# A two-layer graph kernel: the last 20 rows taken as a block of 128, and the third pair of logits parted evenly

## The chip, the cores and the metric

The kernel runs on one core of one Trainium2 chip. The metric is the device time in microseconds (us) of one execution; less is better. A core has the engines TensorE (PE, with its weight load PEld), VectorE (DVE), ScalarE (ACT), GpSimd (POOL) and SyncE (SP, which issues transfers). Each works through its own queue of instructions in order, and the queues meet only at semaphores. On-chip memory is SBUF (128 partitions) and PSUM, where TensorE puts its products.

## The reference

There are N = 2708 nodes with 256 features, an adjacency matrix `adj` (2708 x 2708, some 0.3% of it not zero), and two layers. Everything is 32-bit floating point.

```
x  = layernorm(x + relu([x, adj @ x] @ weight + bias))          # layer 0
R  = (adj + I) / row sums                                       # layer 1
Xf = Xa = x
for n in 0, 1:
    A  = top_p_attention(Xa)     # softmax of q k^T, kept to 0.9 of each row's mass, renormed
    Xf = R @ Xf
    Xa = A @ Xa
    Z  = Z + Xf @ U1[n].T + Xa @ U2[n].T
x  = layernorm(x + layernorm(x + Z) * g + b)
```

with `q = X W1^T W2^T` and `k = X W3^T`, both of 64 features. The attention is over all pairs of nodes: two matrices of 2708 x 2708.

## The kernel before, in words

The nodes are cut into NB = 22 blocks: 21 of 128 rows and one, EDGE, of 20 (2708 = 21 x 128 + 20). `rows(k)` gives 128 or 20. A product over all nodes is 22 matmuls that add up in PSUM, the last one over 20 rows only. Each 32-bit matmul appears in the trace as two MATMUL and two LDWEIGHTS records.

Stages, in time: up to 28 us x is projected to `y0` (L392 to L399). **Layer 0** (28 to 285 us) goes over blocks m: `adj_product` (L257) multiplies 22 tiles of adj, loaded by SP, with `y0`; then comes the projection of x itself (L462), and DVE does relu and layernorm. Every fourth block `x1_qk` (L426) makes the queries q and the keys. Keys of even chunks of 512 columns lie on partitions 0 to 63, those of odd chunks on 64 to 127, so that the two matmuls of a pair of logits use different rows of the array. Six chunks make three pairs, the third of 512 and 148 columns.

Meanwhile DVE collects which columns of each adjacency block are not empty, and `Lists.end` (L325 to L348) turns these lists into indices: a transfer out and in, then seven scatters by POOL (L345), each after the one before has landed, and a load of the result, `ix<-list_d` (L348). There are two such lists; the first comes between layer 0 and the attention.

**Step 0 of the attention** (286 to 722 us). `begin1` starts blocks 0 to 2: logits (`logits`, L507) are copied by ACT (L514) to a row block `e`, with projections by U1 (L651) between. `extract1` (DVE: L570, L577, L579) finds the largest logits, `exps1` (ACT: L611, L613) makes exponentials, and `finish1` (DVE: L627 to L640) cuts at 0.9 of the mass. Then, for each block t, six turns g: `turn` transposes four blocks of e (L527), ACT copies them to `wT` (L530, and L533 for the 20-row one), and `products`, one turn later, multiplies them with x1 (L564). The last turn has two blocks, 20 and 21; its products come in the next block's first turn. Between them stand the logits of block t+3. The order is the program's, written out by hand; no scheduler changes it. POOL gathers pieces of adj (L367).

**Step 1** (from 748 us) has periods `per` of the same kind: transposes, products with `ya` (L564 again), the logits of a later block (L507), a search for the threshold on ACT (L966, L969) and DVE (L1023, L1030, L1083, L1088), and, between them in equal parts, the sparse products R @ X (`r_units`, L749). For these POOL gathers rows by index (`y_load`, L719), seven gathers per block, into two buffers, one block ahead. From about 1047 us POOL also does part of the final normalization (L1207, L1208), which waits for ACT's L1192.

The line of the product in a turn:

```
nc.tensor.matmul(acc[:p, :D], lhsT=wT[:kw, k % 4, :p], rhs=y[:kw, k, :],
                 start=k == 0, stop=k == NB - 1)
```

with kw = 20 where k = 21. For the EDGE block of step 1, `edge_product` (L544 to L550) does all in one.

Of the kernel before, what the change touches and what calls it, by code (L numbers as in the profile page):

```python
# [38 lines left out]
CAP = 160  # L39
ML = 16  # L40
CW, CC = 128, 7


def chunks(N):
    return [(a, min(N, a + CH)) for a in range(0, N, CH)]


class Common:
# [3 lines left out]
@with_exitstack  # L52
def gnn_two_layer_kernel(ctx: ExitStack, tc: tile.TileContext, N, xT_d, x_d, adj_d, w0_d, b0_d,
                         w1_d, w2_d, w3_d, u1_d, u2_d, g_d, b_d, out_d):

    nc = tc.nc
    D = x_d.shape[1]
    DA = w1_d.shape[1]  # L80
    NB = (N + P - 1) // P
    DC = D // P
    assert N % 2 == 0 and NB % 2 == 0 and N * 2.0 ** -15 < 0.09 and DC == 2 and DA == 64
    assert SEG * (NS - 1) + 8 <= N <= SEG * NS == SEG2 * NS2 and N >= SEG2 * (NS2 - 1) + 8
    assert NB == 3 * KS + 1 and CW == P and CAP % 8 == 0 and N < NB * P
# [63 lines left out]
def fast_path(ctx, tc, c, flags, fint, xT_d, x_d, w0_d, b0_d, w1_d, w2_d, w3_d, u1_d, u2_d, g_d, b_d):  # L149
# [97 lines left out]
    def adj_product(acc, m, y, n, stop):  # L247
        p = rows(m)
        halves = adj_of.pop(m)
        for k in range(NB):  # L250
            kw = rows(k)
            if m == EDGE:
                o = EW * (k % 4)
                nc.tensor.matmul(acc[o:o + p, :n], lhsT=halves[k // KH][:kw, k % KH, :p], rhs=y[:kw, k, :n],
                                 start=k < 4, stop=k >= NB - 4)
                continue
            nc.tensor.matmul(acc[:p, :n], lhsT=halves[k // KH][:kw, k % KH, :p], rhs=y[:kw, k, :n],  # L257
                             start=k == 0, stop=stop and k == NB - 1)


# [141 lines left out]


    q = big.tile([P, N], FP, tag="Q", name="q")
    keys = [big.tile([P, (len(CHS) + 1) // 2, CH], FP, tag=f"K{s}", name=f"k{s}") for s in range(2)]


    wqkq = small.tile([P, DC, 3, DA], FP, tag="wqkq", name="wqkq", bufs=1)
# [10 lines left out]
    def qk_project(s, a, b, src):  # L419


        n, i, h = b - a, a // CH // 2, a // CH % 2
        po = ps_misc()
        for j in range(DC):
            w = wqkq[:, j, 1 - h:3 - h].rearrange("p h a -> p (h a)")
            nc.tensor.matmul(po[:, :n], lhsT=w, rhs=src(j), start=j == 0, stop=j == DC - 1)  # L426
        own, other = (slice(DA * g, DA * g + DA) for g in (h, 1 - h))
        nc.scalar.copy(q[other, a:b], po[other, :n])
        nc.scalar.copy(q[own, a:b], po[other, :n])
        nc.scalar.copy(keys[s][own, i, a % CH:a % CH + n], po[own, :n])  # L430

    x1T = big.tile([P, DC, N], FP, tag="B", name="x1T")

# [63 lines left out]
    NL = (len(CHS) + 1) // 2  # L497

    def logits(s, t, i):


        p = rows(t)
        lg = ps_lg()
        cs = CHS[2 * i:2 * i + 2]
        for h, (a, b) in enumerate(cs):
            o = slice(DA * h, DA * h + DA)
            nc.tensor.matmul(lg[:p, h, :b - a], lhsT=q[o, t * P:t * P + p], rhs=keys[s][o, i, :b - a],  # L507
                             start=True, stop=True)
        a, b = cs[0][0], cs[-1][1]
        return lg.rearrange("p h n -> p (h n)")[:p, :b - a], a, b  # L510

    def logits1(t, i):
        lg, a, b = logits(0, t, i)
# [4 lines left out]
    NG = (NB + 3) // 4  # L518
    before = []

    def turn(t, g, y, acc, e):
        p = rows(t)
        ks = range(4 * g, min(NB, 4 * g + 4))
        tr = ps_tr()
        for k in ks:
            kw = rows(k)
            nc.tensor.transpose(tr[:kw, k % 4, :p], e[:p, k * P:k * P + kw], ident[:p, :p])  # L527
        wT = work.tile([P, 4, P], FP, tag="wT", name="wT", bufs=3)
        full = sum(rows(k) == P for k in ks)
        nc.scalar.copy(wT[:, :full, :p], tr[:, :full, :p])  # L530
        if full < len(ks):
            kw = rows(ks[full])
            nc.scalar.copy(wT[:kw, full, :p], tr[:kw, full, :p])  # L533
        before.append((p, ks, wT, y, acc))

    def edge_product(y, acc, e):

        p = rows(EDGE)
        tr = ps_tr().rearrange("p k i -> p (k i)")[:, :NB * p].rearrange("p (k i) -> p k i", i=p)
        wT = work.tile([P, 4, P], FP, tag="wT", name="wT", bufs=3)  # L540
        wT = wT.rearrange("p k i -> p (k i)")[:, :NB * p].rearrange("p (k i) -> p k i", i=p)
        for k in [NB - 1] + list(range(NB - 1)):
            kw = rows(k)
            nc.tensor.transpose(tr[:kw, k, :], e[:p, k * P:k * P + kw], ident[:p, :p])  # L544
        for a, b, kw in ((0, NB - 1, P), (NB - 1, NB, rows(NB - 1))):
            nc.scalar.copy(wT[:kw, a:b, :], tr[:kw, a:b, :])
        for k in range(NB):
            kw = rows(k)
            o = EW * (k % 4)
            nc.tensor.matmul(acc[o:o + p, :D], lhsT=wT[:kw, k, :], rhs=y[:kw, k, :],  # L550
                             start=k < 4, stop=k >= NB - 4)

    def products(keep):

        if len(before) > keep:
            p, ks, wT, y, acc = before.pop(0)
            for k in ks:
                kw = rows(k)
                if p < P:
                    o = EW * (k % 4)  # L560
                    nc.tensor.matmul(acc[o:o + p, :D], lhsT=wT[:kw, k % 4, :p], rhs=y[:kw, k, :],
                                     start=k < 4, stop=k >= NB - 4)
                    continue
                nc.tensor.matmul(acc[:p, :D], lhsT=wT[:kw, k % 4, :p], rhs=y[:kw, k, :],  # L564
                                 start=k == 0, stop=k == NB - 1)

    def seg_max(dst, src, p, step, width):
# [94 lines left out]
    def ya_pair():  # L662
# [11 lines left out]
        if rows(t0 + 1) == P:  # L674
            nc.scalar.copy(ya[:, t0:t0 + 2, :], pz)
            return
        for s in range(2):
            nc.scalar.copy(ya[:rows(t0 + s), t0 + s, :], pz[:rows(t0 + s), s, :])

    def step1_out(t, acc, ra):  # L680

# [215 lines left out]
    for t in range(NB):  # L897
# [6 lines left out]
        for g in range(NG):  # L904
# [16 lines left out]
            if g == 2:  # L921
# [813 lines left out]
```

## Time and profile before

| | |
|---|---|
| median of 3 runs | 1295.33 us (1294.3 to 1296.72) |
| profiled execution | 1291.2 us, of which the span of instructions 1289.4 |
| PE busy | 1226.3 us, 95% of the span |
| PEld, DVE, ACT, POOL busy | 888.1, 973.9, 735.5, 635.9 us |
| chain that ended last | PE 79%, DVE 8%, ACT 7%, DMA 3%, POOL 2% |
| products of 20 rows | 42 records each at L257 and in both steps of L564 |
| third pairs of logits (512 and 148 columns) | 22 in each step |

A row of a timeline gives the start in us, the length in us, the engine, the line, the operation, what is written `<-` what is read, the shape (for PE `rows*columns` of the array, then the moving operand) and how many instructions were merged. In brackets stands how long the engine was idle before, and what ended that; "issue" is nothing that the profile shows. Matmuls overlap, so the time that one takes of the engine is read from start to start, not from its own length.

### The profile page before, as it was taken

To read this page: it belongs to the slowest core of one execution; us is meant where nothing else is said; L and a number is where in the kernel's file an instruction comes from. 1 tells how busy PE (TensorE), PEld (TensorE's weight loads), DVE (VectorE), ACT (ScalarE), POOL (GpSimd) and SP (SyncE) were. 2 spreads that over 40 slices of the span, in tenths; PEclk is the share of its full clock that TensorE was granted. 3 is DMA by queue.
4 is the path that set the end of the run, shared out by engine and by line. 5 is a ranking of instruction groups with operands and counts; after the bars stand their busy time and mean duration, and the time that the engine had idled before them with its cause. 6 is when DMAs were issued, how large, how long until landed. Compare 5 with 4: busy or idle time off the path is not lost.

```text
span 1289.4 us, 18741 instructions
## 1 busy us (share of the span) xinstructions
PE 1226.3 (95%) x5764; PEld 888.1 (69%) x5764; DVE 973.9 (76%) x3252; ACT 735.5 (57%) x1337; POOL 635.9 (49%) x594
## 2 busy tenths in 40 slices
PE   8999999979899999999999987999999999999885
PEld 6878777843477777777777555777766777767664
DVE  2445545884999997977872179889888999999886
ACT  2000110125456656556655488887888989989822
POOL 1000000003475452577756058878874878888860
PEclk9999999999999999999999988999999999999998
DMA  7455445423322210122224244565563545565451
GB/s 196 152 193 170 143 149 168 149 90 107 121 82 83 72 57 28 43 88 91 93 85 100 63 149 150 178 189 177 180 154 118 179 155 154 165 195 158 145 139 39
DMA packets 101703, 165.99 MB, mean 129 GB/s; under 512 B 17362, under 2 KB 74070, under 8 KB 101594
## 3 DMA queue, kind: packets, MB, share of 16 engines
q1 hardware_dynamic: 75308, 108.65, 26.0%
q0 software_dynamic: 20544, 51.17, 14.3%
q10 hardware_dynamic: 5742, 4.89, 1.3%
q8 instruction: 48, 0.79, 0.2%
q14 instruction: 61, 0.50, 0.1%
HBM read 130.74 MB, written 33.90 MB: 128 GB/s over the span
## 4 chain that ended last, share of the span: by engine, by line
PE 79%; DVE 8%; ACT 7%; DMA 3%; POOL 2%; issue 2%; ACTq 0%; POOLq 0%; DVEq 0%
PE acc L564 27%; PE acc L257 16%; PE lg L507 9%; PE misc L749 8%; PE tr L527 7%; PE acc L651 2%; DMA yg<-v_d,ix 2%; PE acc L462 2%; PE misc L392 2%; PE misc L426 2%; PE acc L672 2%; ACT e L966 2%; PE misc L699 1%; DVE e L1088 1%; ACT e L844 1%
## 5 line engine op out<-in xcount | busy, mean ns | idle before, releaser
L530 ACT COPY wT<-tr 128x512 f32<-128x512 f32 (+2 forms) x258 | 132.1, 519 | 208.7 <-PE tr L527 208.7
L564 PE MATMUL acc<-x,wT 128*128 128x256 f32 (+1 forms) x924 | 230.5, 388 | 0.0
L564 PE MATMUL acc<-ya,wT 128*128 128x256 f32 (+1 forms) x924 | 227.1, 385 | 0.0
L719 POOL DMA_INDIRECT yg<-v_d,ix x154 | 194.8, 1265 | 59.6 <-issue 22.6
L564 PEld LDWEIGHTS acc<-x,wT 128*128 128x128 f32 (+1 forms) x924 | 165.2, 189 | 71.0 <-issue 37.4
L719 POOL DMA_INDIRECT yg<-yf_d,ix x154 | 188.2, 1222 | 48.3 <-issue 22.5
L257 PE MATMUL acc<-y,adj_t 128*128 128x257 f32 (+1 forms) x924 | 208.4, 381 | 0.0
L564 PEld LDWEIGHTS acc<-ya,wT 128*128 128x128 f32 (+1 forms) x924 | 170.2, 190 | 44.4 <-issue 24.0
L749 PE MATMUL misc<-yg,adj_t 128*128 128x256 f32 (+1 forms) x704 | 183.7, 394 | 14.9 <-DMA yg<-v_d,ix 5.9
L367 POOL DMA_INDIRECT adj_t<-in_adj,ix x154 | 171.3, 1112 | 52.0 <-issue 41.8
L257 PEld LDWEIGHTS acc<-y,adj_t 128*128 128x128 f32 (+1 forms) x924 | 171.8, 189 | 32.7 <-issue 8.9
L749 PEld LDWEIGHTS misc<-yg,adj_t 128*128 128x128 f32 (+1 forms) x704 | 123.6, 189 | 67.6 <-issue 23.4
L507 PE MATMUL lg<-k,q 64*128 64x512 f32 (+3 forms) x528 | 149.5, 594 | 13.7 <-ACT e L848 7.0
L527 PE MATMUL tr<-ident,e 128*128 128x128 f32 (+2 forms) x946 | 147.1, 274 | 3.1 <-DVE e L1088 2.0
L527 PEld LDWEIGHTS tr<-ident,e 128*128 128x128 f32 (+2 forms) x946 | 112.2, 138 | 44.8 <-issue 16.4
L334 POOL DMA_DIRECT2D part_d<-e x1 | 0.6, 573 | 285.6 <-DVE e L333 285.6
L439 ACT COPY x1T<-tr 128x256 f32<-128x256 f32 (+1 forms) x22 | 8.0, 364 | 186.6 <-PE tr L438 186.6
L966 ACT ACTIVATE e<-e,st 128x2708 f32<-128x2708 f32 (+1 forms) x43 | 113.5, 2639 | 0.1
L969 ACT ACTIVATE e<-e,st 128x2708 f32<-128x2708 f32 (+1 forms) x42 | 110.9, 2641 | 0.1
L570 DVE MAX8 cand<-e 128x8 f32<-128x170 f32 (+1 forms) x352 | 87.2, 318 | 26.7 <-ACT e L514 26.7
L1030 DVE MAX8 cand<-w 128x8 f32<-128x170 f32 (+1 forms) x352 | 94.2, 321 | 0.0
L1083 DVE MATCH_REPLACE8 w<-part,e 128x680 f32<-128x680 f32 (+1 forms) x88 | 74.3, 851 | 0.0
(238 smaller groups left out, 1696.4 us busy)
## 6 DMA issues: line engine op xcount, KB each, us to landing
adj_t<-in_adj SPq DMA_DIRECT2D x44, 704.0 KB
adj_t<-adjc_d SPq DMA_DIRECT2D x44, 448.0 KB
adjc_d<-adj_t SPq DMA_DIRECT2D x22, 256.0 KB
base<-za_d SPq DMA_DIRECT2D x40, 128.0 KB
adjc_d<-adj_t SPq DMA_DIRECT2D x22, 192.0 KB
xt<-in_x ACTq DMA_DIRECT2D x21, 128.0 KB
x_d<-x SPq DMA_DIRECT2D x21, 128.0 KB
x1b_d<-xb SPq DMA_DIRECT2D x21, 128.0 KB
```

The lines of the kernel that those rows point to most:

```text
L257: nc.tensor.matmul(acc[:p, :n], lhsT=halves[k // KH][:kw, k % KH, :p], rhs=y[:kw, k, :n], start=k == 0, stop=stop and k == NB - 1)
L367: nc.gpsimd.indirect_dma_start(out=a[:CW, i, :], out_offset=None, in_=adj_rows, in_offset=bass.IndirectOffsetOnAxis(ap=ix[:CW, m, i:i + 1] ...
L507: nc.tensor.matmul(lg[:p, h, :b - a], lhsT=q[o, t * P:t * P + p], rhs=keys[s][o, i, :b - a], start=True, stop=True)
L527: nc.tensor.transpose(tr[:kw, k % 4, :p], e[:p, k * P:k * P + kw], ident[:p, :p])
L530: nc.scalar.copy(wT[:, :full, :p], tr[:, :full, :p])
L564: nc.tensor.matmul(acc[:p, :D], lhsT=wT[:kw, k % 4, :p], rhs=y[:kw, k, :], start=k == 0, stop=k == NB - 1)
L570: nc.vector.max(dst[:p, i * 8:(i + 1) * 8], src[:p, i * step:i * step + w])
L719: nc.gpsimd.indirect_dma_start(out=y[:CW, i, :], out_offset=None, in_=rows_d, in_offset=bass.IndirectOffsetOnAxis(ap=ix[:CW, m, i:i + 1], ...
L749: nc.tensor.matmul(acc[:p, :D], lhsT=a[:kw, k, :p], rhs=y[:kw, k, :], start=k == 0, stop=k == CC)
L966: nc.scalar.activation(scr[:b.p, :N], e, AF.Relu, bias=b.nz, scale=b.l[k], accum_out=b.relu)
L969: nc.scalar.activation(scr[:b.p, :N], e, AF.Sign, bias=b.nz, scale=b.l[k], accum_out=b.sign)
L1030: nc.vector.max(b.cand[:p, 8 * i:8 * i + 8], low[:p, SEG2 * i:SEG2 * (i + 1)])
```

## The change

1. In layer 0, `y0`'s last block gets zeros (a memset by POOL), and `adj_product` multiplies all 128 rows of the last block.
2. In the attention the last column block is taken as columns 2592 to 2720 of `e` instead of the 20 from 2688. Its 20 real rows are then rows 96 to 115 of the transpose (AT = 96); the rest meets zeros in the other factor. For step 0 that factor is a new piece `x1_edge`, zeroed by POOL and filled with 20 rows by DVE, both after `lists.end()`; for step 1 it is `ya`'s last block, zeroed by POOL at (t, g) = (2, 0) of step 0. ACT copies both transposes of the last turn in one instruction.
3. The third pair of logits is parted into 330 and 330 columns (`key_parts`); the projections that cross the new border at 2378 are parted (columns 2048 to 2560 in layer 0, block 18 in step 0).

```diff
+def key_parts(N):
+    parts = []
+    for a in range(0, N, 2 * CH):
+        b = min(N, a + 2 * CH)
+        parts += [(a, (a + b) // 2), ((a + b) // 2, b)]
+    return parts
...
-            nc.tensor.matmul(acc[:p, :n], lhsT=halves[k // KH][:kw, k % KH, :p], rhs=y[:kw, k, :n],
+            nc.tensor.matmul(acc[:p, :n], lhsT=halves[k // KH][:, k % KH, :p], rhs=y[:, k, :n],
                              start=k == 0, stop=stop and k == NB - 1)
...
     y0 = big.tile([P, NB, D + 1], FP, tag="V", name="y0")
+    nc.gpsimd.memset(y0[:, NB - 1, :D], 0.0)
...
     def qk_project(s, a, b, src):
+        for c_, (ka, kb) in enumerate(KPS):
+            lo, hi = max(a, ka), min(b, kb)
+            if lo >= hi:
+                continue
...
     lists.end()
...
+    x1_edge = y_room[:, YW + 4 * D:YW + 5 * D]
+    nc.gpsimd.memset(x1_edge, 0.0)
+    nc.vector.tensor_copy(x1_edge[AT:AT + rows(EDGE)], x1[:rows(EDGE), EDGE, :])
     lists = Lists(ML, NB, flags[:, NF - 2:], yg[:, 1].rearrange("p c d -> p (c d)"))
...
-        cs = CHS[2 * i:2 * i + 2]
+        cs = KPS[2 * i:2 * i + 2]
+        skip = CH - (cs[0][1] - cs[0][0])
...
+    def columns(e, k):
+        a = min(k * P, NW - P)
+        return e[:, a:a + P]
+
+    def part_y(y, k):
+        return y[:, k, :] if k < NB - 1 or y is ya else x1_edge
...
         for k in ks:
-            kw = rows(k)
-            nc.tensor.transpose(tr[:kw, k % 4, :p], e[:p, k * P:k * P + kw], ident[:p, :p])
+            nc.tensor.transpose(tr[:, k % 4, :p], columns(e[:p], k), ident[:p, :p])
         wT = work.tile([P, 4, P], FP, tag="wT", name="wT", bufs=3)
-        full = sum(rows(k) == P for k in ks)
-        nc.scalar.copy(wT[:, :full, :p], tr[:, :full, :p])
-        if full < len(ks):
-            kw = rows(ks[full])
-            nc.scalar.copy(wT[:kw, full, :p], tr[:kw, full, :p])
+        nc.scalar.copy(wT[:, :len(ks), :p], tr[:, :len(ks), :p])
...
-                nc.tensor.matmul(acc[:p, :D], lhsT=wT[:kw, k % 4, :p], rhs=y[:kw, k, :],
+                nc.tensor.matmul(acc[:p, :D], lhsT=wT[:, k % 4, :p], rhs=part_y(y, k),
                                  start=k == 0, stop=k == NB - 1)
...
+            if (t, g) == (2, 0):
+                nc.gpsimd.memset(ya[:, NB - 1, :], 0.0)
```

More of the change, by code (lines that the diff above doesn't have):

```diff
@@ L41 @@
 CW, CC = 128, 7
+AT = 96
 def chunks(N):
     return [(a, min(N, a + CH)) for a in range(0, N, CH)]
+def key_parts(N):
[4 more added lines that the diff above has]
+    return parts
 class Common:
@@ L84, in gnn_two_layer_kernel @@
     assert SEG * (NS - 1) + 8 <= N <= SEG * NS == SEG2 * NS2 and N >= SEG2 * (NS2 - 1) + 8
+    assert SEG * NS - P == (NB - 1) * P - AT and AT + N - (NB - 1) * P <= P
     assert NB == 3 * KS + 1 and CW == P and CAP % 8 == 0 and N < NB * P
@@ L250, in adj_product @@
         for k in range(NB):
-            kw = rows(k)
             if m == EDGE:
                 o = EW * (k % 4)
-                nc.tensor.matmul(acc[o:o + p, :n], lhsT=halves[k // KH][:kw, k % KH, :p], rhs=y[:kw, k, :n],
+                nc.tensor.matmul(acc[o:o + p, :n], lhsT=halves[k // KH][:, k % KH, :p], rhs=y[:, k, :n],
                                  start=k < 4, stop=k >= NB - 4)
                 continue
-            nc.tensor.matmul(acc[:p, :n], lhsT=halves[k // KH][:kw, k % KH, :p], rhs=y[:kw, k, :n],
+            nc.tensor.matmul(acc[:p, :n], lhsT=halves[k // KH][:, k % KH, :p], rhs=y[:, k, :n],
                              start=k == 0, stop=stop and k == NB - 1)
@@ L404, in fast_path @@
     q = big.tile([P, N], FP, tag="Q", name="q")
-    keys = [big.tile([P, (len(CHS) + 1) // 2, CH], FP, tag=f"K{s}", name=f"k{s}") for s in range(2)]
+    KPS = key_parts(N)
+    keys = [big.tile([P, len(KPS) // 2, CH], FP, tag=f"K{s}", name=f"k{s}") for s in range(2)]
     wqkq = small.tile([P, DC, 3, DA], FP, tag="wqkq", name="wqkq", bufs=1)
@@ L419, in qk_project @@
     def qk_project(s, a, b, src):
[L422 to L430, printed above, removed]
+        for c_, (ka, kb) in enumerate(KPS):
+            lo, hi = max(a, ka), min(b, kb)
+            if lo >= hi:
+                continue
+            n, i, h = hi - lo, c_ // 2, c_ % 2
+            po = ps_misc()
+            for j in range(DC):
+                w = wqkq[:, j, 1 - h:3 - h].rearrange("p h a -> p (h a)")
+                nc.tensor.matmul(po[:, :n], lhsT=w, rhs=src(j)[:, lo - a:hi - a], start=j == 0, stop=j == DC - 1)
+            own, other = (slice(DA * g, DA * g + DA) for g in (h, 1 - h))
+            nc.scalar.copy(q[other, lo:hi], po[other, :n])
+            nc.scalar.copy(q[own, lo:hi], po[other, :n])
+            nc.scalar.copy(keys[s][own, i, lo - ka:hi - ka], po[own, :n])
     x1T = big.tile([P, DC, N], FP, tag="B", name="x1T")
@@ L495, in fast_path @@
     x1_qk(len(CHS) - 1)
-    NL = (len(CHS) + 1) // 2
+    NL = len(KPS) // 2
     def logits(s, t, i):
@@ L503, in logits @@
         lg = ps_lg()
-        cs = CHS[2 * i:2 * i + 2]
+        cs = KPS[2 * i:2 * i + 2]
+        skip = CH - (cs[0][1] - cs[0][0])
         for h, (a, b) in enumerate(cs):
             o = slice(DA * h, DA * h + DA)
-            nc.tensor.matmul(lg[:p, h, :b - a], lhsT=q[o, t * P:t * P + p], rhs=keys[s][o, i, :b - a],
+            at = (skip, 0)[h]
+            nc.tensor.matmul(lg[:p, h, at:at + b - a], lhsT=q[o, t * P:t * P + p], rhs=keys[s][o, i, :b - a],
                              start=True, stop=True)
         a, b = cs[0][0], cs[-1][1]
-        return lg.rearrange("p h n -> p (h n)")[:p, :b - a], a, b
+        return lg.rearrange("p h n -> p (h n)")[:p, skip:skip + b - a], a, b
     def logits1(t, i):
@@ L525, in turn @@
         for k in ks:
-            kw = rows(k)
-            nc.tensor.transpose(tr[:kw, k % 4, :p], e[:p, k * P:k * P + kw], ident[:p, :p])
+            nc.tensor.transpose(tr[:, k % 4, :p], columns(e[:p], k), ident[:p, :p])
         wT = work.tile([P, 4, P], FP, tag="wT", name="wT", bufs=3)
-        full = sum(rows(k) == P for k in ks)
-        nc.scalar.copy(wT[:, :full, :p], tr[:, :full, :p])
-        if full < len(ks):
-            kw = rows(ks[full])
-            nc.scalar.copy(wT[:kw, full, :p], tr[:kw, full, :p])
+        nc.scalar.copy(wT[:, :len(ks), :p], tr[:, :len(ks), :p])
         before.append((p, ks, wT, y, acc))
@@ L541, in edge_product @@
         wT = wT.rearrange("p k i -> p (k i)")[:, :NB * p].rearrange("p (k i) -> p k i", i=p)
[L542 to L546, printed above, removed]
         for k in range(NB):
-            kw = rows(k)
+            nc.tensor.transpose(tr[:, k, :], columns(e[:p], k), ident[:p, :p])
+        nc.scalar.copy(wT, tr)
+        for k in range(NB):
             o = EW * (k % 4)
-            nc.tensor.matmul(acc[o:o + p, :D], lhsT=wT[:kw, k, :], rhs=y[:kw, k, :],
+            nc.tensor.matmul(acc[o:o + p, :D], lhsT=wT[:, k, :], rhs=part_y(y, k),
                              start=k < 4, stop=k >= NB - 4)
@@ L557, in products @@
             for k in ks:
-                kw = rows(k)
                 if p < P:
                     o = EW * (k % 4)
-                    nc.tensor.matmul(acc[o:o + p, :D], lhsT=wT[:kw, k % 4, :p], rhs=y[:kw, k, :],
+                    nc.tensor.matmul(acc[o:o + p, :D], lhsT=wT[:, k % 4, :p], rhs=part_y(y, k),
                                      start=k < 4, stop=k >= NB - 4)
                     continue
-                nc.tensor.matmul(acc[:p, :D], lhsT=wT[:kw, k % 4, :p], rhs=y[:kw, k, :],
+                nc.tensor.matmul(acc[:p, :D], lhsT=wT[:, k % 4, :p], rhs=part_y(y, k),
                                  start=k == 0, stop=k == NB - 1)
@@ L676, in ya_pair @@
             return
-        for s in range(2):
-            nc.scalar.copy(ya[:rows(t0 + s), t0 + s, :], pz[:rows(t0 + s), s, :])
+        nc.scalar.copy(ya[:, t0, :], pz[:, 0, :])
+        p = rows(t0 + 1)
+        nc.scalar.copy(ya[AT:AT + p, t0 + 1, :], pz[:p, 1, :])
     def step1_out(t, acc, ra):
```

## The prediction

> **What bounds the kernel now.** I read the windows by stage first, then the timeline of TensorE (PE) and of its weight load (PEld), then each engine's timeline where PE stood still. The windows (columns: length, then busy us and count of PE, PEld, DVE, ACT, POOL, then clock, DMA share, GB/s):
> ```profile
> 28.40:270.00 241.60, 240.08 (x1069) 194.24 (x1067) 136.46 (x323) 21.92 (x56) 0.00 (x0) 1.00 0.49 160
> 359.39:657.56 298.17, 298.17 (x1497) 216.02 (x1496) 255.45 (x951) 179.73 (x340) 174.27 (x171) 1.00 0.23 71
> 810.26:953.00 142.74, 141.88 (x681) 107.12 (x681) 121.24 (x418) 118.51 (x197) 114.69 (x93) 1.00 0.61 184
> 1047.60:1246.70 199.10, 189.56 (x892) 140.35 (x892) 185.88 (x645) 171.15 (x300) 164.87 (x145) 0.99 0.54 166
> ```
> Layer 0 (first row) and attention step 0 (second) are PE from end to end: what PE saves there is saved outright. In step 1 PE is nearly full too, but others are close. The weight-load timeline of one stretch of step 0 shows what a 20-row product costs:
> ```profile
> 500.76 0.30 PEld L564 LDWEIGHTS acc<-x,wT 128*128 128x128 f32 x2 [0.76 <-ACT wT L530]
> 501.39 0.29 PEld L564 LDWEIGHTS acc<-x,wT 20*128 20x128 f32 x2 [0.33 <-issue]
> 502.02 0.42 PEld L527 LDWEIGHTS tr<-ident,e 128*128 128x128 f32 x4 [0.33 <-issue]
> 502.60 0.30 PEld L507 LDWEIGHTS lg<-k,q 64*128 64x128 f32 x4 [0.17 <-issue]
> ```
> The loader, which otherwise runs ahead under the matmuls, stands still for 0.33 us with nothing to wait for when the rows go from 128 to 20, and 0.33 again on the way back. (Each product is two records, as all are here.) Layer 0 has the same, and a row without such a change gives the plain rate:
> ```profile
> 59.10 1.22 PE L257 MATMUL acc<-y,adj_t 128*128 128x257 f32 x4
> 60.25 1.13 PE L462 MATMUL acc<-e,xT 128*128 128x256 f32 x4
> 61.22 0.38 PE L438 MATMUL tr<-ident,x 128*128 128x128 f32 x2
> 495.50 1.89 PE L564 MATMUL acc<-x,wT 128*128 128x256 f32 x8
> 497.23 0.38 PE L527 MATMUL tr<-ident,e 128*128 128x128 f32 x2
> ```
> Eight full records take 497.23-495.50 = 1.73, so 0.216 each.
>
> **What the skill says.** "TensorEngine Tiling (Array Packing)", Key Properties: changing the tiling mode drains the engine. The trace agrees: 0.33 idle of the loader at each change. "TensorE: Matmul & The Clock Gate", LDWEIGHTS (loading the stationary operand): the time goes by columns, not by rows. Agrees: the loads of L564 take 181 to 192 ns, 20 rows or 128. The same page, "Architectural detail", says that VectorE's queue is strict first-in-first-out; no run here shows it yet, and Part 4 rests on it. Its Part 1 says that an idle TensorE falls to half its clock: eight records of L651 took 5.46 us after a wait of 3.91, against 3.70.
>
> **Part 1: 20 rows filled to 128, layer 0.** Two full and two 20-row records, 59.10 to 60.25, take 1.15 where four full ones take 0.864: 0.29. The four L462 behind them take 0.97 for 0.864: 0.10 for the way back. 0.39 for each of 21 blocks = 8.2; the 20-row block 21 changes mode as well, about 0.2 by estimate. The memset of y0 costs nothing: POOL is idle before 28 us, 108x256 takes 0.30. Faster PE does not run into the loads: a block's first half is issued 7.6 us before it is needed (204.67 for 212.23) and its packets are through by about 209. **-8.4**; the split projection of columns 2048 to 2560 adds 0.1.
>
> **Part 2: the same in step 0.** The four L564 at 500.77 start with two full ones, the 20-row pair at 501.39; from the pair to the transposes at 502.02 is 0.63 where two full records take 0.43, the way in costs 0.09, and the first transpose behind takes 0.16 where later ones take 0.11: 0.20+0.09+0.05 = 0.34. 21 pairs: 7.2, and 0.2 in the edge block. The 20-column transposes cost as much as full ones (0.11), so filling them costs nothing. ACT's two copies (0.27+0.25) become one of 128x256, about 0.38 by L439: a small gain, hidden. **-7.4**; block 18's projection, parted at 2378, adds four records at 0.11: +0.4.
>
> **Part 3: 330 and 330.** The two halves of a pair run at the same time on 64 rows each: the pair 512+512 at 499.71 takes 1.06 to the next row, and 512+148 at 506.24 also 1.06. So the shorter half is free and the longer sets the time. By the record of 256 columns, 0.216, a column is 0.84 ns; two passes of 182 columns fewer are 0.31, less 0.01 by which 148 was better: 0.30. Nothing shows a 330-column record: no gain at worst, 0.30 at best, and I take 0.30, since 512 and 257 columns keep one rate. 19 pairs within step 0: **-5.6**; three before step 1 (733.95 to 748): **-0.9**; three at the start of step 0 fall to the wait below.
>
> **Part 4: the new wait.** x1_edge is zeroed on POOL and then filled by DVE. In the changed program's order the memset stands behind the whole first list chain, after ix<-list_d, and the DVE copy, which waits for it, stands right before the first L570. Before:
> ```profile
> 297.78 0.21 DVE L341 SCALAR_TENSOR_TENSOR to<-run,before_m,e 16x7 int32<-16x7 f32 x1
> 297.92 3.86 DVE L570 MAX8 cand<-e 128x8 f32<-128x170 f32 x16
> 320.36 0.21 DVE L627 TENSOR_SCALAR sc<-z 128x1 f32<-128x1 f32 x1 [10.73 <-ACT e L613]
> 316.11 1.24 POOL L348 DMA_DIRECT2D ix<-list_d  x1 [1.40 <-DMA list_d<-e,to]
> 317.35 0.11 POOL L584 MEMSET xs<- 128x1 f32 x1
> 317.17 0.35 ACT L611 ACTIVATE srt<-srt,nmax 128x65 f32<-128x65 f32 x1
> ```
> POOL is free at 317.35 (seven scatters, each waiting for the last one's landing); the memset takes 0.3 to 0.4, the copy 0.2 to 0.4, so the first L570 starts at about 318.1, 20.2 late. Queued behind it is block 0's ordering; it ends at 307.3 now and is needed by ACT's L611 at 317.17. So 9.9 of the 20.2 are covered by ACT's queue and 10.3 go through: L611 starts at 327.5, then L613, DVE's L627 and the ordering of block 1, which is also what PE waits for at 338 (3.91). PE stands at 321.3 for those 10.3 and then falls to half clock; that costs 2 to 3 us, which fits under the 3.91. From 8.5 (the later drop to half clock falls away) to 11: **+10.3**.
>
> **Part 5: step 1.** A period has one 20-row pair and one third pair, 0.64 of 23.78. But the sparse product L749 needs gathers by POOL, seven to a block:
> ```profile
> 871.58 3.56 POOL L719 DMA_INDIRECT yg<-yf_d,ix  x1 [0.30 <-DMA yg<-yf_d,ix]
> 875.45 0.95 POOL L719 DMA_INDIRECT yg<-yf_d,ix  x1 [0.30 <-issue]
> 958.37 0.70 PE L749 MATMUL misc<-yg,adj_t 128*128 128x256 f32 x2 [0.20 <-DMA yg<-yf_d,ix]
> 1047.58 0.73 POOL L1207 TENSOR_TENSOR yg<-yg,gb 128x256 f32<-128x256 f32 x1 [2.79 <-ACT yg L1192]
> PE misc L749 <- DMA yg<-v_d,ix: 5.9, 9, 1.3
> ```
> POOL issues them every 1.25 us without a pause from 750 to 965, two of a period taking 3.3 to 3.6; at 958 PE already waits for one. So up to there POOL's pace holds, and PE's gain turns into that wait. The same from 1047.58 (where POOL has 2.79 to spare) to 1246.7, where PE waits 5.9 for gathers. Kept are: one period after 958, 0.6; 998.8 to 1047.6, PE full, 2.1 periods, 1.35; the tail after 1246.7, PE full from 1255, two pairs and the edge, 0.8. **-2.8** (0 to -13.6 if nothing held). The memset of ya, 0.3 us between gathers of step 0, has 380 us to spare.
>
> **Sum.** -8.4+0.1-7.4+0.4-5.6-0.9+10.3-2.8 = -14.3. Against the profiled execution, 1291.2 (span 1289.4 and 1.8 around it), 1276.9; the median of the three runs is 1295.33, 4.1 above it, and the forecast is 1295.3-14.3 = 1281.
>
> **Rivals.**
> - Step 1 keeps its gain (0.14): PE's speed would also have to speed up POOL. For it: slack of 1 to 5 us at most blocks. Against: POOL without a pause. 20 periods at 0.64 and the tail are 13.6: 1270.
> - The stall does not appear, because POOL's list chain is early or the copy is not in the way (0.07): 1271. Against: the order in both queues.
> - The stall passes in full, 20.2 (0.12), if work that I count as cover moves with it: 1291.
> - Slower: filling the rows does not remove the change of mode, so the gap belongs to the end of an accumulation and not to 20 rows (0.05). Parts 1, 2 and the pairs in Part 5 lose 17.2: +2.9, 1298. It decides once a filled pair saves less than about 0.06 instead of 0.34 to 0.39. Against: no gap where 128-row products of different blocks follow each other.
>
> **Numbers.** The forecast has 0.62, its own range 1277 to 1287. With the first two rivals, 0.83: 1270 to 1287. Within 0.2% (about what this kernel's runs can tell from no change) 0.03, slower 0.04, faster 0.93.
>
> **What would show it.** PEld without the 0.33 at L257 and L564; layer 0's period 10.64 for 11.03; step 0's 16.9 for 17.54; the third pair 0.76 for 1.06; the first L570 some 20 us after L341; POOL's gathers still every 1.25 us and more PE wait for yg. A DVE that goes on at once after L341, or no added wait for yg, would make it wrong.

## The result, and the profile after

The changed kernel takes 1283.25 us (median of 4 runs, 1278.78 to 1286.8), the kernel before 1295.01 (4 runs, 1294.3 to 1296.72): ratio 0.9904, 95% interval 0.9883 to 0.9926. Beside the later experiments it ran again: 1281.65 (1276.87 to 1285.06) against 1296.69, ratio 0.9892, interval 0.9877 to 0.9908. The forecast was 1281, with a range of 1277 to 1287. The profiled execution of the first set took 1286.8, its slowest; that of the second 1276.87, its fastest, and 14.3 less than the profiled execution before (1291.2). I use both below, as the first and the second profile of the changed kernel.

Two lines of part 1 and two groups of part 5 of the first page. The last figure of a group is the idle time that its main releaser ended:
```profile
span 1284.9 us, 18709 instructions
...
PE 1202.1 (94%) x5772; PEld 904.3 (70%) x5772; DVE 973.9 (76%) x3253; ACT 735.1 (57%) x1299; POOL 634.9 (49%) x597
...
L769 PE MATMUL misc<-yg,adj_t 128*128 128x256 f32 (+1 forms) x704 | 187.9, 398 | 18.1 <-DMA yg<-yf_d,ix 7.2
...
L266 PEld LDWEIGHTS acc<-y,adj_t 128*128 128x128 f32 x924 | 174.9, 191 | 27.3 <-issue 1.9
```
TensorE works 24 us less (1226.3 before), but the span is only 4.5 shorter: the difference went into waits. The loader's idle time that nothing explains ("issue") fell at the layer-0 product from 8.9 to 1.9. Before:
```profile
L257 PEld LDWEIGHTS acc<-y,adj_t 128*128 128x128 f32 (+1 forms) x924 | 171.8, 189 | 32.7 <-issue 8.9
```
That is 7.0, or 21 gaps of 0.33: the way into the 20-row pair, once a block. The 21 gaps of the way back stood at the next product (7.0 at L462) and are gone too (L477).

The windows of the same stages as before, shifted with the work (length, then busy us and count of PE, PEld, DVE, ACT, POOL, then clock, DMA share, GB/s):
```profile
28.66:263.74 235.08, 233.56 (x1069) 199.19 (x1069) 136.09 (x323) 21.93 (x56) 0.00 (x0) 0.99 0.50 163
363.14:650.46 287.32, 287.32 (x1498) 219.21 (x1497) 255.01 (x951) 178.97 (x323) 171.39 (x170) 1.00 0.24 73
805.86:948.84 142.98, 140.47 (x681) 107.53 (x680) 121.75 (x422) 118.51 (x191) 115.25 (x92) 1.00 0.61 183
1042.50:1240.95 198.45, 185.59 (x892) 141.96 (x892) 186.86 (x648) 171.13 (x293) 163.88 (x144) 0.99 0.55 167
```
Layer 0 is 6.5 shorter (first row), with a short stretch at half clock in it; its ordinary block takes 10.65 in both profiles, where it took 11.03. Step 0 (second row) is still TensorE without a pause, and 10.9 shorter over 17 blocks: 0.64 each, as forecast. The two stretches of step 1 last about as long as before (142.74 and 199.10), with less of TensorE in them: 2.5 and 12.9 us of it idle, where it was 0.9 and 9.5.

The weight-load timeline around a filled pair of step 0, and after it the TensorE timeline of a third pair (330 and 330), both of the first profile. `x1_edge` lies in the room of `yg`, so the profile calls it `yg`: the second row is the filled pair.
```profile
499.41 0.30 PEld L583 LDWEIGHTS acc<-x,wT 128*128 128x128 f32 x2 [0.76 <-ACT wT L556]
499.73 0.41 PEld L583 LDWEIGHTS acc<-yg,wT 128*128 128x128 f32 x2
500.16 0.58 PEld L554 LDWEIGHTS tr<-ident,e 128*128 128x128 f32 x4
500.91 0.30 PEld L527 LDWEIGHTS lg<-k,q 64*128 64x128 f32 x4 [0.17 <-issue]
```
```profile
289.45 0.83 PE L527 MATMUL lg<-k,q 64*128 64x330 f32 x4
290.20 1.98 PE L670 MATMUL acc<-u,x1T 128*128 128x512 f32 x4
```
The gaps of 0.33 around the 20-row pair are gone with the pair. The third pair takes 290.20-289.45 = 0.75 to the next row, where 512 and 148 columns took 1.05 (from 297.79 in the profile before): the 0.30 of the forecast.

The new wait, in the timelines of VectorE, GpSimd and ScalarE:
```profile
291.42 0.21 DVE L350 SCALAR_TENSOR_TENSOR to<-run,before_m,e 16x7 int32<-16x7 f32 x1
311.22 0.56 DVE L509 COPY yg<-x 20x256 f32<-20x256 f32 x1 [19.58 <-POOL xs L603]
311.79 3.88 DVE L589 MAX8 cand<-e 128x8 f32<-128x170 f32 x16
...
309.63 1.24 POOL L357 DMA_DIRECT2D ix<-list_d  x1 [1.41 <-DMA list_d<-e,to]
310.86 0.32 POOL L508 MEMSET yg<- 128x256 f32 x1
...
321.22 0.35 ACT L630 ACTIVATE srt<-srt,nmax 128x65 f32<-128x65 f32 x1 [12.88 <-DVE srt L596]
```
VectorE stands still for 19.58 before its copy, until GpSimd's memset of `x1_edge` (L508; the profile names the memset next to it, L603) is done, and the first MAX8 starts 20.36 after L350 where it was 0.14.

The start of the same VectorE instruction against the profile before, in us, worked out from the traces (the last column is the experiment e8 told below, with VectorE's memset):
```
place (its time before)          first    second   attention filled only
layer 0, end        (274.49)     -7.09    -8.96    +0.26
first MAX8          (297.92)    +13.87   +10.80    +2.08
first exps, L627    (320.36)     +4.05    +0.98    +1.30
step 0, last MAX8   (662.50)     -7.45   -12.16    -4.87
step 1, start       (767.55)     -5.84   -12.24    -5.95
step 1, middle      (985.77)     -3.75   -11.78    -7.07
step 1, later      (1088.35)     -5.40   -13.46    -7.86
step 1, end        (1266.25)     -5.61   -13.87    -8.47
```

### The profile page after: what moved, and what is told of

Read it like the earlier page. It is cut to its first block, busy times and chain, and to the rows that moved or that the text cites. A ratio compares the mean times of both kernels' runs of the same rounds, so it can differ in the third digit from the quotient of the medians.

```text
span 1284.9 us, 18709 instructions
## 1 busy us (share of the span) xinstructions
PE 1202.1 (94%) x5772; PEld 904.3 (70%) x5772; DVE 973.9 (76%) x3253; ACT 735.1 (57%) x1299; POOL 634.9 (49%) x597
## 4 chain that ended last, share of the span: by engine, by line
PE 71%; DVE 10%; ACT 7%; DMA 6%; issue 3%; POOL 2%; SPq 0%; POOLq 0%; ACTq 0%; DVEq 0%
PE acc L583 23%; PE acc L266 16%; PE lg L527 8%; PE misc L769 6%; PE tr L554 6%; DMA yg<-yf_d,ix 3%; PE acc L670 2%; DMA yg<-v_d,ix 2%; DVE e L1110 2%; PE misc L402 2%; ACT e L988 2%; PE acc L691 2%; PE misc L441 2%; PE misc L719 2%; PE acc L477 1%
## 5 line engine op out<-in xcount | busy, mean ns | idle before, releaser
L583 PE MATMUL acc<-ya,wT 128*128 128x256 f32 x924 | 223.1, 383 | 0.0
L583 PE MATMUL acc<-x,wT 128*128 128x256 f32 x882 | 217.4, 386 | 0.0
L266 PE MATMUL acc<-y,adj_t 128*128 128x257 f32 x924 | 206.1, 382 | 0.0
L583 PEld LDWEIGHTS acc<-x,wT 128*128 128x128 f32 x882 | 159.0, 190 | 58.1 <-issue 24.7
L583 PEld LDWEIGHTS acc<-ya,wT 128*128 128x128 f32 x924 | 172.1, 191 | 38.2 <-issue 16.7
L266 PEld LDWEIGHTS acc<-y,adj_t 128*128 128x128 f32 x924 | 174.9, 191 | 27.3 <-issue 1.9
L769 PEld LDWEIGHTS misc<-yg,adj_t 128*128 128x128 f32 (+1 forms) x704 | 123.6, 191 | 69.6 <-issue 23.2
L527 PE MATMUL lg<-k,q 64*128 64x512 f32 (+3 forms) x528 | 138.0, 600 | 27.4 <-ACT e L534 13.5
L554 PE MATMUL tr<-ident,e 128*128 128x128 f32 (+1 forms) x946 | 145.2, 272 | 6.9 <-ACT wT L556 4.6
L554 PEld LDWEIGHTS tr<-ident,e 128*128 128x128 f32 (+1 forms) x946 | 117.7, 141 | 40.5 <-ACT wT L556 8.8
L527 PEld LDWEIGHTS lg<-k,q 64*128 64x128 f32 (+1 forms) x528 | 39.3, 183 | 59.1 <-issue 20.7
```

Of the source, the lines that this page charges most:

```text
L266: nc.tensor.matmul(acc[:p, :n], lhsT=halves[k // KH][:, k % KH, :p], rhs=y[:, k, :n], start=k == 0, stop=stop and k == NB - 1)
L527: nc.tensor.matmul(lg[:p, h, at:at + b - a], lhsT=q[o, t * P:t * P + p], rhs=keys[s][o, i, :b - a], start=True, stop=True)
L554: nc.tensor.transpose(tr[:, k % 4, :p], columns(e[:p], k), ident[:p, :p])
L583: nc.tensor.matmul(acc[:p, :D], lhsT=wT[:, k % 4, :p], rhs=part_y(y, k), start=k == 0, stop=k == NB - 1)
L769: nc.tensor.matmul(acc[:p, :D], lhsT=a[:kw, k, :p], rhs=y[:kw, k, :], start=k == 0, stop=k == CC)
```

## The experiments

My theory was that of the prediction: filled pairs save 0.39 and 0.34, a third pair 0.30, the memset behind the list chain costs about 10.5, and GpSimd's gathers take the gain of step 1. The rivals were those on record there.

The chips differ, and this has to be known to read the numbers: in the first two sets the kernel before took 1345.09 and 1342.36, in the third 1296.69 as in the result. The changed kernel as it is (second profile above) ran beside the third set:

> The changed kernel as it is, beside the kernel before on a chip of these experiments. The chips of the experiments gave 1342 to 1345 us for the kernel before, with pauses of ScalarE, and there the version with VectorE's memset had a ratio of 0.976 to 0.981. My theory: the stall costs 10 us there too, so the changed kernel stands 0.007 to 0.008 above that version: ratio 0.984 to 0.988, with the first MAX8 some 20 us behind L350. Rival 'where ScalarE pauses, part of the stall is hidden by them': ratio 0.978 to 0.982, as good as the version without it.

Measured 0.9892; but the chip was not one of those that the expectation speaks of. On the two slow chips ScalarE stops now and then with nothing late that the trace shows ("remote" is a release by nothing that the trace holds). The ScalarE timeline of the kernel before with only layer 0 filled:
```profile
347.48 0.19 ACT L613 ACTIVATION_READ_ACCUMULATOR e<-e,nmax 128x1 f32 x1
351.19 0.58 ACT L530 COPY wT<-tr 128x512 f32<-128x512 f32 x1 [3.52 <-remote]
351.67 1.38 ACT L613 ACTIVATE e<-e,nmax 128x1300 f32<-128x1300 f32 x1
```
The transposes that it copies had ended at 347.46. From the first logits to the first sparse product TensorE's idle stretches of over 0.15 us add up to 21 to 29 us in six traces of those chips, and to 25 and 36 in the two with the stall alone (some 10.5 of it the stall), against 8.9 in the profile before. The stops are not spread at random: all eight traces of the two chips have one of 5.8 to 8.6 us at the same copy of 512 columns, the last one for block 20 of step 0, where the profile before idles for 0.96. So totals are compared within a chip, and the parts by traces.

**VectorE zeroes x1_edge**, in the changed kernel (e1, e1b).
```diff
-    nc.gpsimd.memset(x1_edge, 0.0)
+    nc.vector.memset(x1_edge, 0.0)
```


> The changed kernel with one word changed: x1_edge is zeroed by VectorE instead of GpSimd. My theory (the GpSimd memset stands behind the first list chain, and the VectorE copy that waits for it holds up the first MAX8 of block 0; 10.7 us of that go through): VectorE goes on within 1 us of L350, the stage from the first logits to step 0 takes about 57 us again instead of 67.4, and the kernel takes 1273 us, 10 below the changed one. Rival 'the stall passes in full': 20 us come back, 1263. Rival 'the stall is covered, and the longer stage has another cause, such as TensorE at half clock': below 2 us come back, 1281 to 1283.

1319.57 against 1345.09, ratio 0.981 (0.9766 to 0.9854). Repeated:

> The changed kernel with x1_edge zeroed by VectorE, once more: the first try was on a chip on which the kernel before took 1345 us, with pauses of ACT, VectorE and TensorE that no instruction released and that the first two profiles do not have. My theory: without such pauses 10 us less than the changed kernel, 1273 us; ratio to before 0.983. The stage from the first logits to the first block of step 0 takes 57 us, not 67.4. Rival 'the part of the stall that is passed on is partly taken back later, because step 1 follows GpSimd': 5 to 7 us come back, 1276 to 1278, ratio 0.986.

1312.85 against 1342.36, ratio 0.976 (0.9735 to 0.9785). The stall is gone in both. The VectorE timeline of the same edit with fewer gathers, on the third chip (see below):
```profile
289.46 0.21 DVE L350 SCALAR_TENSOR_TENSOR to<-run,before_m,e 16x7 int32<-16x7 f32 x1
289.67 0.27 DVE L508 MEMSET yg<- 128x256 f32 x1
289.98 0.29 DVE L509 COPY yg<-x 20x256 f32<-20x256 f32 x1
290.27 3.88 DVE L589 MAX8 cand<-e 128x8 f32<-128x170 f32 x16
```
0.82 from L350 to the first MAX8. The distance from the start of that instruction to the first MAX8, and to ScalarE's first exponential behind the ordering, in all traces:
```
                                          to MAX8    to first exp
before                                     0.14       19.39
no new wait (e3, e4, e4b, e6b)             0.14       18.60 to 19.46
VectorE's memset (e1, e1b, e5, e6a, e8)    0.82       18.60 to 20.08
GpSimd's memset, changed (two profiles)   20.12, 20.36   29.56, 29.80
GpSimd's memset alone (e2, e2b)           20.56, 20.76   30.00, 30.20
```
The wait is this one, and of its 20 us 10.2 to 10.8 pass on. The 10.2 to 10.8 are counted from the 19.39 of the kernel before; without the wait that distance itself varies by some 1.5. The totals do not say by themselves what it costs at the end, since the changed kernel ran on other chips: its ratios are 0.989 and 0.990.

**The stall alone**, in the kernel before (e2, e2b).
```diff
+    x1_edge = y_room[:, YW + 4 * D:YW + 5 * D]
+    nc.gpsimd.memset(x1_edge, 0.0)
+    nc.vector.tensor_copy(x1_edge[96:96 + rows(EDGE)], x1[:rows(EDGE), EDGE, :])
```


> The kernel before with only the two new instructions put in, the GpSimd memset of x1_edge and the VectorE copy into it, at the same place; their result is read by nobody. My theory: the wait of about 19.6 us appears in VectorE's queue, 10 to 11 us of it reach the end: 1305.5 us. Rival 'in full': 1315. Rival 'covered': 1295 to 1296.

1352.08, ratio 1.004 (1.002 to 1.006). Repeated:

> The kernel before with only the two new instructions (GpSimd memset of x1_edge, VectorE copy), once more. In the first try 10.6 us passed through the stage, but the end was only 5.6 us later. My theory: where ACT and TensorE have no pauses of their own, 10 us reach the end, ratio 1.008. Rival 'step 1 takes half back': 5 us, ratio 1.004, with the difference at 10 us up to step 1 and shrinking in it.

1346.9, ratio 1.0033 (1.0013 to 1.0053). 10.6 to 10.8 us pass through the place; only 7 and 4.5 reach the end by the medians, 5.4 and 4.4 by the ratios. The half of the repeat's rival is what was measured, and not the 10 of my theory, but on chips whose ScalarE stops anyway; which later wait absorbs the rest I could not tell, since two executions there differ by as much.

**Layer 0 filled alone**, in the kernel before (e3).
```diff
+    nc.gpsimd.memset(y0[:, NB - 1, :D], 0.0)
...
-            nc.tensor.matmul(acc[:p, :n], lhsT=halves[k // KH][:kw, k % KH, :p], rhs=y[:kw, k, :n],
+            nc.tensor.matmul(acc[:p, :n], lhsT=halves[k // KH][:, k % KH, :p], rhs=y[:, k, :n],
```

> The kernel before with only the filling of the rows in layer 0. My theory: 0.39 us for each of 21 blocks, 8.2 to 8.4 in all, unless short waits at half clock take 1 to 2 of it: 1286.5 to 1288.5 us; the loader's idle time at the layer-0 product put down to issue falls from 8.9 to about 2 us. Rival 'the gap belongs to the end of an accumulation, not to the 20 rows': 1295, the 8.9 stay. Rival 'TensorE runs into the loads of the next block or what layer 0 gains is lost behind it': 1292 to 1295, with waits for adj_t.

1337.95, ratio 0.9927 (0.9901 to 0.9952): 7 us less by the medians and 10 by the ratio, where 8.4 was forecast. A group of part 5, and the same of the kernel with only the attention filled, in which layer 0 is as before:
```profile
L256 PEld LDWEIGHTS acc<-y,adj_t 128*128 128x128 f32 x924 | 173.7, 189 | 26.8 <-issue 1.9
```
```profile
L267 PEld LDWEIGHTS acc<-y,adj_t 128*128 128x128 f32 (+1 forms) x924 | 171.8, 189 | 32.7 <-issue 8.9
```
The gap goes with the 20 rows although the accumulations end where they did, so the slower rival falls. This fits "TensorEngine Tiling (Array Packing)" in the Trainium skill, Key Properties, which says that a change of mode drains the engine (that a 20-row product counts as another mode is my reading). The price is not one constant. At a change between 128 and 20 rows behind products of 256 columns the loader stands for 0.33 us; at the changes between 128 rows and the 64 of the logits, in the profiles before and after, for 0.17 behind matmuls of 128 columns, 0.33 behind 256, 0.46 behind 330 and 0.76 behind 512 (medians). These changes remain in the changed kernel.

**330 and 330 alone**, in the kernel before (e4, e4b): keys, projections and logits by `key_parts` as in the change, nothing filled.
```diff
-        cs = CHS[2 * i:2 * i + 2]
+        cs = KPS[2 * i:2 * i + 2]
+        skip = CH - (cs[0][1] - cs[0][0])
```

> The kernel before with only the third pair of logits parted into 330 and 330 (and the projections that this parts). My theory: 22 pairs in and around step 0 save 0.30 us each, of which 19 and 3 count (6.6), the parted projection of block 18 gives back 1.2, and of the 20 pairs of step 1 (6.0) about 1 is kept, because GpSimd's gathers set the pace there: 1288 to 1290 us. Rival 'step 1 keeps its gain': 1283 to 1284. Rival 'the pair goes by the sum of its columns, and 330+330 is no shorter than 512+148': 1296.

1331.41, ratio 0.9889 (0.9855 to 0.9923). Repeated:

> The kernel before with only the third pair of logits at 330 and 330, once more. In the first try it saved 15 us in place of 6, and I put the rest down to the pauses of that chip. My theory: 5 to 7 us here, ratio 0.995, with 0.30 a period in step 0. Rival 'the parting saves more than its matmuls, since ACT and VectorE get the last columns earlier': 12 to 15 us, ratio 0.989.

1332.73, ratio 0.9903 (0.9876 to 0.9929): 14 and 10 us by the medians, 15 and 13 by the ratios, more than the 5 to 7 expected. The rival of the repeat is nearer. On those chips a part that frees TensorE saves more than its matmuls; no run tells why, and the parting was not tried alone on a chip without the pauses.

**The attention filled alone**, in the kernel before, with VectorE's memset (e5).
```diff
+    x1_edge = y_room[:, YW + 4 * D:YW + 5 * D]
+    nc.vector.memset(x1_edge, 0.0)
+    nc.vector.tensor_copy(x1_edge[AT:AT + rows(EDGE)], x1[:rows(EDGE), EDGE, :])
...
-                nc.tensor.matmul(acc[:p, :D], lhsT=wT[:kw, k % 4, :p], rhs=y[:kw, k, :],
+                nc.tensor.matmul(acc[:p, :D], lhsT=wT[:, k % 4, :p], rhs=part_y(y, k),
```

> The kernel before with only the filling of the last block in the attention, x1_edge zeroed by VectorE. My theory: 21 pairs of step 0 save 0.34 each (7.2), of step 1's 6.8 about 1 is kept, the VectorE memset and copy cost under 1: 1287 to 1288 us, ratio 0.994. Rival 'step 1 keeps its gain': 1281, ratio 0.989. Rival 'the gap belongs to the end of an accumulation': ratio 1.000.

1323.78 against 1342.36, ratio 0.985 (0.9824 to 0.9876): 18.6 us, more than my theory and more than the rival that lets step 1 keep its gain. To see whether ScalarE's merged copy was the surplus, its two copies were put back (e8; in `edge_product` as well):
```diff
-        nc.scalar.copy(wT[:, :len(ks), :p], tr[:, :len(ks), :p])
+        full = sum(rows(k) == P for k in ks)
+        nc.scalar.copy(wT[:, :full, :p], tr[:, :full, :p])
+        if full < len(ks):
+            nc.scalar.copy(wT[:, full, :p], tr[:, full, :p])
```


> The kernel before with the last block filled in the attention, as in the run that gave 0.985, but ScalarE still copies the last two transposes of a block in two instructions instead of one. In that run 18.6 us were saved where the matmuls account for 8 to 14. Theory A (the surplus is ScalarE's merged copy, 0.15 to 0.25 us a block off a chain that TensorE waits for on these chips): 6 to 9 us less are saved, ratio 0.990 to 0.992. Theory B (the surplus is TensorE's own, and ScalarE's copies are hidden as I forecast): ratio 0.984 to 0.987.

1284.52 against 1296.69, ratio 0.9914 (0.9898 to 0.9929). The number is theory A's, but it came from the chip without pauses, where there is no surplus to explain, so it does not decide between the two. What it does show is the size of the fill: in the last column of the table above, from 320.36 to 662.50, 6.17 us in 18 blocks of step 0, 0.34 each, with both copies in place. With the merged copy the changed kernel gains 0.64 a block, which is this 0.34 and the 0.30 of the third pair; so in step 0 the merging adds nothing, as the forecast had it.

**Fewer gathers**, in the changed kernel with VectorE's memset (e6a) and in the kernel before (e6b). From the third block on 3 of 7 gathers are left out, so that the sparse product reads stale rows; their transfers fall away with them:
```diff
-        for i in range(CC):
+        for i in range(CC if m < 2 else 4):
```


> The version with VectorE's memset, with 4 of the 7 gathers of each block from the third on (it leaves out 3/7 of what the sparse product reads, which then uses stale rows; 120 GpSimd gathers of 1.25 us fall away). My theory: GpSimd's gathers hold the pace of step 1, so that without them the whole 13.6 us that TensorE saves in step 1 arrive: this version is about 10 us further from its partner, the kernel before with the same gathers left out, than the two full ones are from each other (29 us): some 35 to 39 us between the two. Rival 'the gathers do not hold the pace; the pauses of ScalarE and VectorE do, or the gain was kept already': the same 25 to 29 us between the two.

1255.04, ratio 0.9676 (0.9663 to 0.9689).

> The kernel before with 4 of the 7 gathers of each block from the third on (it leaves out 3/7 of what the sparse product reads). My theory: TensorE waits 10 us for gathers in step 1 of the full kernel, and is nearly full otherwise, so that 8 to 12 us fall away, ratio 0.991 to 0.994. Rival 'GpSimd's pace is hidden': ratio 0.998 to 1.000. Rival 'GpSimd sets the whole of step 1': 20 us or more, ratio below 0.985.

1285.62, ratio 0.9909 (0.9895 to 0.9922): 11 us, within what my theory said for this kernel. Between the two lie 30.6 us, which is neither my theory's 35 to 39 nor the rival's 25 to 29. The starts of the same VectorE instruction in both, worked out from the traces (in step 1 other instructions than in the table above):
```
                       before, fewer   VectorE's memset, fewer   difference
first MAX8                300.48             290.27                -10.20
step 0, last MAX8         664.95             643.36                -21.59
step 1, start             762.75             738.58                -24.16
                          944.19             915.41                -28.78
                         1051.07            1020.55                -30.51
                         1086.80            1055.02                -31.79
step 1, end              1266.75            1234.95                -31.80
```
Up to 1086.80 TensorE's 0.64 a block now arrives (7.6 us in all; with all gathers the changed kernel gained nothing from 767.55 to 985.77). So the gathers do hold the first half of step 1, by their issue on GpSimd or by their transfers, which the edit does not separate. The kernel before gains nothing there without them (4.5 later than the profile before at 767.55, 5.1 at 985.77): its TensorE was as slow as they were. Behind 1086.80 nothing more is gained, with the gathers out of the way. The windows of two periods there, of the kernel with VectorE's memset and fewer gathers:
```profile
1074.32:1097.51 23.19, 22.57 (x110) 17.35 (x110) 22.44 (x79) 22.25 (x39) 12.90 (x13) 1.00 0.47 148
1120.71:1143.90 23.19, 22.57 (x110) 17.35 (x110) 22.44 (x79) 22.25 (x39) 12.90 (x13) 1.00 0.46 149
```
And of the kernel before with fewer gathers:
```profile
1156.39:1179.59 23.20, 23.19 (x111) 17.14 (x110) 22.45 (x79) 22.30 (x40) 12.92 (x13) 1.00 0.48 150
```
Both periods last 23.2. In the second TensorE is full (23.19). In the first it does 0.62 less and waits 0.61 for ScalarE's wT once a period, while VectorE and ScalarE are busy 22.4 and 22.3 of it. So the next limit is not TensorE's work but the loop in which ScalarE and VectorE wait for one another and for TensorE, at the same 23.2; which link of it holds the rest these windows do not show, and no run tried it.

## Why the prediction was right, step by step

**Parts 1 to 3, the sizes.** All three held: 0.39 a block in layer 0, 0.34 for a filled pair in step 0, 0.30 for a third pair. Forecast for layer 0 was -8.3 with the split. The first profile shows -6.7 at the first logits (280.07 for 286.76), the second -8.6 (278.15). Most of the difference is one half-clock window. Block 0 of layer 0 in TensorE's timeline, first profile and second:
```profile
28.66 11.51 PE L266 MATMUL acc<-y,adj_t 128*128 128x257 f32 x44
40.01 1.02 PE L477 MATMUL acc<-e,xT 128*128 128x256 f32 x4
```
```profile
28.47 9.83 PE L266 MATMUL acc<-y,adj_t 128*128 128x257 f32 x44
38.14 1.03 PE L477 MATMUL acc<-e,xT 128*128 128x256 f32 x4
```
The same 44 records take 11.35 and 9.67: behind two waits of 0.44 and 0.48 the clock was halved from 28.7 for 3.4 us in the one and not in the other. One reading was too wide: the prediction gives 0.33 for each change of rows, but its own line at 502.60, a change from 128 to 64 rows, has 0.17. Its sums take no price from such a change, so they stand. From the first exponentials to the start of step 1 the forecast was -13.5 (Part 2, its +0.4 and both figures of Part 3); measured -9.9 and -13.2. Of the 3.3 between the two, 1.6 come from a half-clock window (342.8 to 346.2) that the second profile does not have, and 1.4 from one (708.0 to 714.8) that is half as long there.

One term was too small: block 18's parted projection, taken as +0.4 for its four records. It also takes both buffers of "misc" one after the other, so TensorE waits for ScalarE's copy out of the first. PE's waits, first profile:
```profile
PE lg L527 <- ACT e L534: 13.5, 2, 13.0
PE misc L769 <- DMA yg<-yf_d,ix: 7.2, 10, 2.8
PE misc L769 <- DMA yg<-v_d,ix: 7.2, 9, 1.2
...
PE misc L719 <- ACT k L445: 0.5, 1, 0.5
```
The last line is that wait, the only one at L719. With it the parting costs 1.1 in both profiles, by the same instructions' starts on either side of it.

**Part 4, the wait.** Forecast: first MAX8 20.2 late, 9.9 of it covered, 10.3 passed on. Measured: 20.2 later (20.36 for 0.14), 10.4 passed on to the first exponential, and from the end of layer 0 to L627 11.1 and 9.9 in the two profiles. The copy takes 0.56 there and not 0.2 to 0.4. TensorE stood 13.0 us in the first profile (first line above) and 10.6 in the second, where 10.3 was forecast, and then ran at half clock. The shorter wait behind it (2.4 and 1.2 for 3.91 at L670) gave part of this back, as the forecast said; the later drop to half clock fell away in the second profile only. That VectorE's queue is strictly in order is what "TensorE: Matmul & The Clock Gate" in the Trainium skill, "Architectural detail", states. The trace agrees: while the copy waited 19.58 for GpSimd, the sixteen MAX8 behind it did not start, though their operands were ready (with VectorE's memset they start 0.82 after L350). The rivals (the stall does not appear, or passes in full) are refuted for this place by the table of distances. What 10 us at this place are worth at the end is shown less well: no pair of runs with and without them was made on one chip without the pauses, and with the pauses 4.4 to 7 arrived.

**Part 5, step 1.** Forecast -2.8; from the start of step 1 to its last block +0.2 and -1.6, to the end of the span +1.4 and -2.1. The mechanism of the first half is shown: the gathers. TensorE's waits for them grew from 4.5 and 5.9 (`yf_d` and `v_d`) to 7.2 and 7.2 in the first profile, 6.4 and 6.1 in the second. For the second half the forecast named the gathers alone. They did hold the kernel before there (with fewer of them it gains 10.5 between 1088.35 and 1266.25 against the profile before), but the loop with VectorE and ScalarE stands right behind them at 23.2, so that making TensorE and GpSimd both faster gives that half nothing. The rival that lets step 1 keep its gain had not counted it either: of its 13.6 only 7.6 came without the gathers' pace, and 6.5 were left at the end of the span.

GpSimd's pace is also not its own. The prediction takes the long gathers (two a period, 3.3 to 3.6 us for 0.95) as given. In the profile before and in the second profile after, each of the 41 gathers of over 1.5 us runs beside one VectorE instruction of some 3.04 us (L1023 or L1088, 128x2720; once L635) and ends 0.81 to 0.83 after it, and no gather of ordinary length starts more than 0.03 into such an instruction. The partner of the gather that the prediction shows at 871.58, in VectorE's timeline before:
```profile
871.28 3.04 DVE L1088 SCALAR_TENSOR_TENSOR e<-w,st,e 128x2720 f32<-128x2720 f32 x1
```
Two long gathers a period, at about 2.2 more each, are 4.4 of GpSimd's 23.8. The times fit so closely that VectorE's instruction seems to hold the gather; no run tried it with a shorter one.

**The sum.** -14.3 against the profiled execution gave 1276.9; the second profiled execution took 1276.87, the first 1286.8. To the end of layer 0, the first L627, the start of step 1 and the end of the span the second gives -9.0+9.9-13.2-2.1 = -14.4, near the forecast in every term, and the first -7.1+11.1-9.9+1.4 = -4.5. That the total is met to 0.1 is luck: the second is the fastest of four executions that go up to 1285.06. The 9.9 us between the two are no step's error, since the program is the same. Four half-clock windows that the second lacks or has at half the length make 1.7, 1.6, 1.4 and 1.3 of it (from 28.7, 342.8, 708.0 and 1267.8 in the first), 2.1 arise at the stall, and the rest I have not followed.

## What to carry to other kernels

A fill with zeros removed the change of row mode and paid 0.34 to 0.39 us a pair; it was worth that where TensorE was the only full engine, and next to nothing where gathers or a loop with two other engines ran at the same pace (about 2 us in the whole second half of step 1). The buffer for the fill held the first exponentials back by about 10 us where the whole change gained 12 to 15 (how much of that reaches the end is not settled), because a memset of 0.3 us was put in a queue behind seven dependent scatters, and an in-order engine waited for it: look at what stands ahead of a new instruction in its queue. Here it helped to put it on the engine that uses the result. With VectorE's memset that wait is 0.82 instead of 20 us; against the kernel before, that version measured 0.976 and 0.981, and on a chip like those of the result, where it was not run, it should take 1272 to 1278 (an estimate: 1282 less the 10 that passed on, or less the 4.4 to 7 that reached the end where the stall was put in alone).

## What the runs showed of the hardware that was not expected

Whether a short TensorE wait is followed by half clock varies between executions of one program: the waits of 0.44 and 0.48 at 27 to 28 us were followed by 3.4 us at half clock in one profile and not in the other. Such windows account for some 6 of the 10 us between two executions here, which is as large as most single parts of this change; the kernel before spread by 2.4 us in the first set, the changed one by 8.

Chips differ by more than the change: 1342 to 1345 us and 1295 to 1297 for the same kernel, with ScalarE stopping for 2 to 9 us at a time on the first kind, the longest stop of step 0 each time at the same copy. Where that comes from stays open, and so does why single parts saved up to twice their matmuls there.
